# A graph attention stage beside a small mixture of experts: the order of TensorE, DVE and ACT written out tile by tile

## The chip, the cores and the metric

The kernel runs on one core of one Trainium2 chip. It is one launch that computes four graph layers with a feed-forward layer after each. The metric is the time of one execution on the device in microseconds (us). The time before the change is the median of three runs. Besides these there is one execution taken by the hardware profiler, from which all views come; its own time is given in the table below.

A core has five engines that work beside each other: TensorE (PE, matrix products, with the loading of weights shown apart as PEld), VectorE (DVE), ScalarE (ACT), GpSimd (POOL) and SyncE (SP, which here only issues transfers). TensorE writes to PSUM, from which DVE and ACT read. Engines wait for each other by semaphores.

## The reference

There are N = 3125 nodes with 256 features and E = 53125 edges, sorted by the node `dst` at which they end. The change touches the first graph layer and the feed-forward layer after it; six more layers follow, and each reads the whole result of the one before.

```python
def _L0_gnn_ref(nfeat, attn_bias, Wq, Wk, Wv, Wo, src, dst):
    ...
    q = (nfeat @ Wq.T).reshape(n, HEADS, HEAD_DIM) / SCALING
    k = (nfeat @ Wk.T).reshape(n, HEADS, HEAD_DIM)
    v = (nfeat @ Wv.T).reshape(n, HEADS, HEAD_DIM)
    attn = jnp.einsum('ehd,ehd->eh', k[src], q[dst])
    attn = attn + attn_bias
    m = jax.ops.segment_max(attn, dst, num_segments=n)
    a = jnp.exp(attn - m[dst])
    s = jax.ops.segment_sum(a, dst, num_segments=n)
    a = a / s[dst]
    out = jax.ops.segment_sum(v[src] * a[:, :, None], dst, num_segments=n)
    return out.reshape(n, FEAT) @ Wo.T
...
x = x + _L0_gnn_ref(_layernorm(x, axis=-1), edge_attr_8, L0_gnn_Wq, L0_gnn_Wk, L0_gnn_Wv, L0_gnn_Wo, src, dst)
x = x + _L0_ffn_ref(_layernorm(x, axis=-1)[None], L0_ffn_sW1, ..., L0_ffn_gb)[0]
```

So each edge takes the key and the value of its source node and the query of its target node, in 8 heads of 32; a softmax runs over the edges of a target, and the weighted values are summed by target. The feed-forward layer normalizes a row and adds a shared network of three layers (256, 256, 128, 256) and a mixture of four small experts (256, 128, 64, 256), of which each row keeps the two with the highest gates; their weights are a softmax of these two gates.

## The kernel before

**Tiles.** The 3125 nodes are 25 tiles (`T`) of 125 (`P`). The edges that end in one tile are a window of at most 18 chunks (`WC`) of 128 edges. A window is handled in three pieces of six chunks (`PC`), and a piece is one buffer `kv` of 128 edges by 6 chunks, which holds the weights of the heads, a column of ones, the keys (columns `KO` to `VO`) and the values (from `VO`). Before the loop, keys and values of all nodes are written to memory (`kv_d`).

**What is done for a tile**, with the lines of the kernel before:
- `gathered` (L1660): six indirect transfers by POOL's queue bring the rows of a piece; five may be under way, and each has to follow the fifth before it. There are seven buffers `kv`. DVE then sets the column of ones (L1666).
- `one_hot` (one operation of DVE, L282) marks for each edge its target; SP loads the tile's normalized rows `lt_t` and the edges' biases `eb_t`. `one_hot_turned` turns the marks on TensorE (18 transposes, L1826) and ACT copies them out in three parts (L1827, `oht`).
- `queries` (L1815 to L1819): a product on TensorE, scaled by ACT, and split into three bf16 parts so that their sum is exact: a cast on DVE, a difference on DVE, a cast on ACT, a difference on DVE.
- `logits(p)` for each piece: nine blocks `qx` for a tile, of two chunks each, are products of `oht` and the three query parts (six matmuls, L1840). DVE multiplies the keys by each block (L1843), and per piece sums over each head (L1844). Two PSUM buffers `qx` take turns.
- `sums_of`: DVE adds the bias (L1850), ACT takes a first exponential at an eighth of the size (L1853, `el`), TensorE sums it by target (18 matmuls, L1856), DVE copies (L1858).
- `weights_of`: DVE makes from these sums a level for each target (L1864), TensorE hands it to the edges (18 matmuls, L1868), DVE subtracts and clips (L1869, L1871), ACT takes the exponentials into `kv` (L1873, three).
- `weighted`: for each piece DVE multiplies values by weights (L1878), ACT casts the marks to float (L1883, `oh_f`), TensorE sums six chunks into `acc` (L1885), which has one buffer. The column of ones makes the number of edges `deg` of each target beside it.
- `normed`, `normed_turned`, `projected`: DVE copies `deg` (L1890), takes inverses (L1892, L1893) and scales (`ao`, L1895); TensorE turns it (L1902), ACT copies (L1904), TensorE multiplies by `Wo`, DVE adds to `x` (L1909).

**The loop.** It runs 26 times, t = 0 to 25, and each time works on three tiles: `now` (logits), `before` (the tile ahead of it: weights, values, projection) and `after` (the one behind it: marks and queries). After the loop the counts `deg` are used for the next stages.

**The experts beside it.** A tile whose attention is done is ready for the experts. `Experts0` takes the tiles in pairs, as a generator `group`; each call of `more.step` runs it to its next `yield`, with one buffer for each name and one PSUM buffer `tr`. A pair has 14 steps: normalize (DVE statistics and a square root by ACT, L230 to L242), turn (L250), gates (from L719), turned gates, two halves of `s1`, then `s2`, the experts two by two with `e1`, `pair` and `pick` (L885 is the product with the gates), and the output product and addition to `x` (L893) for each tile. The loop calls `beside()` eight times per iteration. `evacuate` (copies out of PSUM, L224 and L226) and `relu_into` (L779 and L781) go to DVE and ACT in turn. There are 11 pairs inside the loop. `group`'s weights are loaded at its start, and DVE adds two of their biases (L834) before the first pair.

**Windows.** From t = 5 on the loop also calls `windows.next()` once an iteration: steps that prepare indices for later graph stages, among them two indirect transfers on POOL's queue that wait for SP's load of pointers.

**What sets the order.** The program text gives an order, and the tile scheduler of the language decides from it, with estimates of its own, in which order the instructions of each engine are put. So matmuls of the experts, logits and `acc` come out mixed. What is queued on one engine then runs in that fixed order.

Of the kernel before, what the change touches and what calls it, by code (L numbers as in the profile page):

```python
# [10 lines left out]
F32 = mybir.dt.float32  # L11
# [24 lines left out]
H, HD = 8, 32  # L36
# [34 lines left out]
def gnn_ffn_kernel(ctx: ExitStack, tc: tile.TileContext, a, out: bass.AP):  # L71
# [156 lines left out]
    def normalize(pool, dst, src, n, tag, scale=None):  # L228
# [8 lines left out]
        nc.scalar.activation(rs[:, :n], rs[:, :n], AF.Sqrt)  # L237
        nc.vector.reciprocal(rs[:, :n], rs[:, :n])
# [6 lines left out]
    def transposed(psum, dst, src, n, relu=False):  # L245

        for k in range(2):
# [5 lines left out]
            if not relu:  # L253
                evacuate(dst[:, k, :n, :], of)
            elif k:
                nc.scalar.activation(dst[:, k, :n, :], of, AF.Relu)
            else:
                nc.vector.tensor_scalar(dst[:, k, :n, :], of, 0.0, None, ALU.max)

# [458 lines left out]
    def gates(pool, psum, lt, n, wg, bias, ne, top, ahead=None):  # L718


# [20 lines left out]

        nc.vector.tensor_tensor(g, ps[:, :n * ne].rearrange("p (i e) -> p i e", e=ne),
                                bias.unsqueeze(1).to_broadcast([P, n, ne]), ALU.add)
        exp_from_max()
        normed(g)
# [5 lines left out]
        ranks(pool, first, g, n, ne, ahead)  # L751
        nc.vector.tensor_scalar(first, first, 2.5, None, ALU.is_lt)
        if top == "softmax":
            exp_from_max()
        nc.vector.tensor_mul(g, g, first)
# [3 lines left out]
    class TurnedGates:  # L759
# [7 lines left out]
        def __call__(self, psum, g, n, ne):  # L767
# [5 lines left out]
            evacuate(wt[:ne, :n, :].rearrange("e i p -> e (i p)"), ps[:ne, :n * P])  # L773
            return wt

    def relu_into(dst, ps, bias):
        turn[0] ^= 1
        if turn[0]:
            nc.vector.tensor_scalar(dst, ps, bias, 0.0, ALU.add, ALU.max)  # L779
        else:  # L780
            nc.scalar.activation(dst, ps, AF.Relu, bias=bias)  # L781
# [11 lines left out]
    class Experts0:  # L793


        def __init__(self, pools):
# [4 lines left out]
            with weights_of_pool(wpool, (SLOT0, D)):  # L801
                self.group = experts0_by(pool, psum, 2)
# [11 lines left out]
    def experts0_by(pool, psum, most):  # L814
# [30 lines left out]

        def group(t0, n):
            ln = pool.tile([P, most, D], F32, name="ln")
            normalize(pool, ln, x[:, t0:t0 + n, :], n, "a")
            yield
            lt = pool.tile([128, 2, most, P], F32, name="lt")  # L850
            transposed(psum, lt, ln, n)
            yield
            g = gates(pool, psum, lt, n, gw, gb, 4, "softmax", ahead)
            yield
            gt = turned_gates(psum, g, n, 4)
            c = n * P

            def hidden(name, m, terms, bias):
                ps = tr()
                product(ps[:m, :c], terms)  # L860
                relu_into(name, ps[:m, :c], bias)
# [11 lines left out]
            for p in range(2):  # L873
# [8 lines left out]
                relu_into(e2[:, p, :c], ps2[:, :c], cols2[:, p:p + 1])  # L882
                ps = tr()
                product(ps[:, :c], [(pick[:, p, :], fan(gt[:, :n, :]))])
                nc.vector.tensor_mul(e2[:, p, :c], e2[:, p, :c], ps[:, :c])  # L885
                yield
            for i in range(n):
# [4 lines left out]
                        + [(e2[:, p, at], ew3[:, p, :]) for p in range(2)])  # L892
                nc.vector.tensor_add(xt, xt, po)  # L893
                yield
# [732 lines left out]
    def attention(windows, experts):  # L1627
# [10 lines left out]
        with ExitStack() as es:  # L1638
# [16 lines left out]
            def gathered(at):  # L1655
# [10 lines left out]
                nc.vector.memset(kv[:, :, KO - 1:KO], 1.0)  # L1666
# [130 lines left out]
            def one_hot(t):  # L1797
                s = Tile()
                s.t, s.kv = t, begun if t == 0 else []
                oh = pool.tile([128, WC, HC], BF16, name="oh")  # L1800
                one_hots(oh, row_h[:, t * WC:(t + 1) * WC, :], iota_h)
                s.oh = oh[:, :, :P]
# [6 lines left out]
            def queries(s):  # L1809

                ps = psum.tile([P, D], F32, name="sm")
                product(ps, [(s.lt[:, k, :], wq[:, k, :]) for k in range(2)])
                s.q = pool.tile([P, 3, D], BF16, name="q_t")
                q = pool.tile([P, D], F32, name="q")
                nc.scalar.activation(q, ps, AF.Copy, scale=float(HD) ** 0.5)  # L1815
                nc.vector.tensor_copy(s.q[:, 0, :], q)
                nc.vector.tensor_sub(q, q, s.q[:, 0, :])
                nc.scalar.copy(s.q[:, 1, :], q)
                nc.vector.tensor_sub(s.q[:, 2, :], q, s.q[:, 1, :])  # L1819

            def one_hot_turned(s):
                s.oht = pool.tile([P, WC, 128], BF16, name="oht")
                for c0 in range(0, WC, PC):
                    ps = psum.tile([128, 1024], BF16, name="sm")
                    for c in range(PC):
                        nc.tensor.transpose(ps[:P, c * 128:(c + 1) * 128], s.oh[:, c0 + c, :], ident_h)  # L1826
                    nc.scalar.copy(s.oht[:, c0:c0 + PC, :].rearrange("d c e -> d (c e)"),  # L1827
                                   ps[:P, :PC * 128])
                s.l = pool.tile([128, WC, H], F32, name="l")

            def logits(s, p):

                if p == len(s.kv):
                    s.kv.append(gathered(s.t * WC + p * PC))
                kv = s.kv[p]
                for c0 in range(0, PC, 2):
                    ps = psum.tile([128, 2, D], F32, name="qx", bufs=2)
                    for c in range(2):
                        for k in range(3):
                            nc.tensor.matmul(ps[:, c, :], s.oht[:, p * PC + c0 + c, :], s.q[:, k, :],  # L1840
                                             start=(k == 0), stop=(k == 2))
                    k_ = kv[:, c0:c0 + 2, KO:VO]
                    nc.vector.tensor_mul(k_, k_, ps)  # L1843
                nc.vector.tensor_reduce(  # L1844
                    s.l[:, p * PC:(p + 1) * PC, :],
                    kv[:, :, KO:VO].rearrange("p c (h d) -> p c h d", h=H), AX.X, ALU.add)

            def sums_of(s):
# [3 lines left out]
                el = pool.tile([128, WC, H], BF16, name="el")  # L1852
# [666 lines left out]
```

## Time and profile before

| what | us |
|---|---|
| median of three runs | 3411.0 |
| lowest and highest of them | 3409.88, 3411.66 |
| the profiled execution, its time | 3415.6 |
| the profiled execution, its span | 3413.8 |
| from the span's start to the first matmul of the attention (L1840) | 119.5 |
| from there to the last matmul of `acc` (L1885) | 797.3 |
| from there to the span's end | 2497.0 |

The profiler's own time is 0.13% above the median. The span is what the trace covers, from its first to its last instruction.

The next answer gives the busy time of each engine in these three stretches; the number in brackets counts instructions. It is followed by PE's granted clock as a share of full speed, the busy share of the transfer engines and what they moved.

```profile
0.00:119.50 119.50, 71.80 (x241) 37.55 (x242) 62.20 (x231) 23.98 (x60) 31.94 (x40) 0.87 0.65 189
119.50:916.80 797.30, 708.14 (x4621) 550.44 (x4620) 610.90 (x1319) 222.20 (x445) 451.50 (x442) 0.92 0.53 153
916.80:3413.80 2497.00, 2352.99 (x11729) 1858.21 (x11727) 1069.06 (x3358) 787.83 (x1492) 196.53 (x157) 0.96 0.36 98
```

The columns after the stretch and its length are PE, PEld, DVE, ACT and POOL. In the attention stage PE is busy in 708 of 797 us, DVE in 611, POOL in 452, most of it with the gathers, ACT in 222. [...]

The largest groups of that stage, by line, are these; after the bar stand the busy time and the mean of one instruction in ns, then how long the engine was idle just before them and what released it.

```profile
L1885 PE MATMUL acc<-kv,oh_f 128*125 128x265 f32 x900 | 224.9, 412 | 14.6 <-DVE kv L1878 14.6
L1840 PE MATMUL qx<-q_t,oht 125*128 125x256 bf16 x1350 | 216.2, 296 | 53.9 <-DVE kv L1843 41.2 <-DVE q_t L1819 5.7 <-ACT q_t L1818 5.5
...
L1843 DVE TENSOR_TENSOR kv<-kv,qx 128x512 f32<-128x512 f32 x225 | 150.7, 679 | 26.2 <-PE qx L1840 24.7 <-DMA kv<-kv_d,src_w 0.7
...
L1844 DVE TENSOR_REDUCE l<-kv 128x48 f32<-128x1536 f32 x75 | 130.9, 1745 | 0.2
L1878 DVE TENSOR_TENSOR kv<-kv 128x1536 f32<-128x1536 f32 x75 | 128.4, 1750 | 0.6 <-ACT kv L1873 0.6
```

PE stands idle for 53.9 us ahead of logit matmuls, mostly until DVE has freed a block `qx`, and for 14.6 us ahead of `acc`.

### The profile page before, as it was taken

How to read it: one execution, taken by the hardware profiler on the slowest of the kernel's cores; microseconds unless marked ns; L12 is line 12 of the kernel's file. 1: busy time of each engine (PE TensorE's matmuls, PEld its weight loads, DVE VectorE, ACT ScalarE, POOL GpSimd, SP SyncE). 2: the span in 40 equal slices, each digit the busy share in tenths (PEclk: the TensorE clock that was granted, in tenths of full speed). 3: DMA queues.
4: the chain of work that ended last, by engine and by line, in shares of the span. 5: the costliest groups of instructions: out<-in, count | busy, mean ns of one | idle time of the engine just before them, and what ended most of it. 6: DMA issues, size and time to landing. Idle time of an engine off the chain costs nothing. (4 is left out here: it accounts for less than half of the span.)

```text
span 3413.8 us, 45380 instructions
## 1 busy us (share of the span) xinstructions
PE 3132.9 (92%) x16587; PEld 2446.2 (72%) x16587; DVE 1742.2 (51%) x4905; ACT 1034.0 (30%) x1996; POOL 680.0 (20%) x639
## 2 busy tenths in 40 slices
PE   6688998998888899999996999979999999999898
PEld 2466776777677789898885888868755555579666
DVE  6577778777697534344674122155521111355662
ACT  1222332332255423232331222234423232332120
POOL 1665564655100000000134333200000000000000
PEclk9789998999889999999997999989999999999997
DMA  5755554555256734444344666553200000043001
GB/s 165 235 172 150 160 163 143 160 165 144 61 165 215 192 99 119 102 108 110 91 123 133 185 178 180 167 137 103 69 19 10 10 19 10 7 122 100 21 1 39
DMA packets 253208, 388.23 MB, mean 114 GB/s; under 512 B 41454, under 2 KB 201069, under 8 KB 252973
## 3 DMA queue, kind: packets, MB, share of 16 engines
q1 hardware_dynamic: 184090, 226.68, 23.3%
q0 software_dynamic: 54064, 141.25, 15.3%
q10 hardware_dynamic: 14819, 17.27, 1.9%
q8 instruction: 134, 2.20, 0.3%
q14 instruction: 101, 0.83, 0.1%
HBM read 314.47 MB, written 70.58 MB: 113 GB/s over the span
## 5 line engine op out<-in xcount | busy, mean ns | idle before, releaser
L2222 PE MATMUL agg<-cnt_f,hp 125*128 125x500 f32 (+1 forms) x3500 | 733.1, 369 | 22.2 <-ACT hp L2163 22.0
L2222 PEld LDWEIGHTS agg<-cnt_f,hp 125*128 125x128 f32 x3500 | 635.5, 189 | 103.2 <-ACT hp L2163 23.1
L1660 POOL DMA_INDIRECT kv<-kv_d,src_w x450 | 450.9, 1002 | 281.5 <-PE acc L1885 140.5
L2200 ACT CAST cnt_f<-blk 125x500 fp32r<-125x500 bf16 (+1 forms) x435 | 245.5, 565 | 518.4 <-PE agg L2222 496.7
L2200 DVE CAST cnt_f<-blk 125x500 fp32r<-125x500 bf16 (+1 forms) x440 | 185.5, 423 | 265.5 <-PE agg L2222 221.6
L1382 DVE SCALAR_TENSOR_TENSOR x<-po,gall,x 125x256 f32<-125x256 f32 x200 | 93.8, 484 | 417.5 <-PE po L266 416.9
L1376 ACT ACTIVATE h<-hid_ps,shift,scale 128x500 f32<-128x500 f32 (+1 forms) x224 | 161.9, 723 | 376.0 <-PE hid_ps L266 375.5
L1840 PE MATMUL qx<-q_t,oht 125*128 125x256 bf16 x1350 | 216.2, 296 | 53.9 <-DVE kv L1843 41.2
L1885 PE MATMUL acc<-kv,oh_f 128*125 128x265 f32 x900 | 224.9, 412 | 14.6 <-DVE kv L1878 14.6
L1885 PEld LDWEIGHTS acc<-kv,oh_f 128*125 128x125 f32 x900 | 178.5, 201 | 54.2 <-DVE kv L1878 18.5
L1840 PEld LDWEIGHTS <-oht 125*128 125x128 bf16 x1350 | 138.2, 105 | 100.4 <-issue 50.6
L266 PE MATMUL po<-wslot,h 128*125 128x256 f32 x800 | 203.0, 386 | 0.1
L266 PEld LDWEIGHTS po<-wslot,h 128*125 128x125 f32 x800 | 145.0, 187 | 75.2 <-ACT h L1376 27.0
L266 PE MATMUL hid_ps<-h,wslot 128*128 128x500 f32 (+1 forms) x448 | 193.8, 556 | 4.1 <-ACT h L1376 0.6
L266 PE MATMUL hid_ps<-xe,wslot 128*128 128x256 f32 x832 | 187.3, 383 | 1.8 <-DVE xe L1214 1.8
L1072 POOL DMA_INDIRECT xs_d<-r_l,pos x50 | 60.2, 1204 | 645.3 <-DVE r_l L1068 567.1
L266 PE MATMUL hid_ps<-v_rows,wslot 128*128 128x500 f32 (+1 forms) x448 | 186.8, 537 | 0.0
L1225 ACT ACTIVATE hid<-hid_ps,wslot 128x256 f32<-128x256 f32 x208 | 98.5, 475 | 286.8 <-PE hid_ps L266 286.8
L266 PE MATMUL po<-wslot,hid 128*128 128x256 f32 x832 | 184.5, 378 | 0.0
L266 PEld LDWEIGHTS hid_ps<-xe,wslot 128*128 128x128 f32 x832 | 150.7, 191 | 33.4 <-ACT hid L1225 4.1
L266 PEld LDWEIGHTS po<-wslot,hid 128*128 128x128 f32 x832 | 155.7, 189 | 21.8
L1843 DVE TENSOR_TENSOR kv<-kv,qx 128x512 f32<-128x512 f32 x225 | 150.7, 679 | 26.2 <-PE qx L1840 24.7
(512 smaller groups left out, 4625.8 us busy)
## 6 DMA issues: line engine op xcount, KB each, us to landing
wslot<-in_ex_W SPq DMA_DIRECT2D x52, 1024.0 KB
blk<-an_d SPq DMA_DIRECT2D x60, 546.9 KB
blk<-at_d SPq DMA_DIRECT2D x40, 546.9 KB
blk<-an_d SPq DMA_DIRECT2D x45, 410.2 KB
at_d<-ab SPq DMA_DIRECT2D x25, 683.6 KB
an_d<-an SPq DMA_DIRECT2D x25, 683.6 KB
blk<-at_d SPq DMA_DIRECT2D x30, 410.2 KB
kv<-kv_d,src_w POOLq DMA_INDIRECT x450, 3.7
```

The source lines that it names most:

```text
L266: nc.tensor.matmul(ps, l, r, start=(bias is None and i == 0), stop=(i == last))
L1072: st = nc.gpsimd.indirect_dma_start(out=xs_d, in_=l2[:, i, :].bitcast(I32), in_offset=None, out_offset=bass.IndirectOffsetOnAxis(ap=self.p ...
L1225: nc.scalar.activation(hid[:, m, :], ps[:, :BLK], AF.Gelu, bias=c[:, 4 + m:5 + m])
L1376: nc.scalar.activation(dst[:, m, :c], ps[:, :c], AF.Relu, bias=shift[:, l, col:col + 1], scale=scale[:, l, col:col + 1])
L1382: nc.vector.scalar_tensor_tensor(x[:, t0 + i, :], po, gating.all[:, t0 + i, e:e + 1], x[:, t0 + i, :], ALU.mult, ALU.add)
L1660: got = nc.gpsimd.indirect_dma_start(out=kv[:, c, KO:], out_offset=None, in_=kv_d, in_offset=bass.IndirectOffsetOnAxis(ap=src_i[:, at + c: ...
L1840: nc.tensor.matmul(ps[:, c, :], s.oht[:, p * PC + c0 + c, :], s.q[:, k, :], start=(k == 0), stop=(k == 2))
L1843: nc.vector.tensor_mul(k_, k_, ps)
L1885: nc.tensor.matmul(s.acc[:, :D + H + 1], of[:, c, :], kv[:, c, AO:VO], start=(p == 0 and c == 0), stop=(p == 2 and c == PC - 1))
L2200: to(f[:, :n, :], part[0][:, :n, m % MB, :])
L2222: nc.tensor.matmul(ps[f][:, :c], hp[:, m, k, f * 128:(f + 1) * 128], got[:, :c], start=(m == 0 and k == 0), stop=(m == T - 1 and k == 1))
```

## The change

The attention loop is put inside `tc.manual_schedule` for PE, DVE and ACT: on these three engines the order of the program text is the order in which instructions are queued. POOL's and SP's queues are not named in it. The text of an iteration is new, as the function `iteration(t, b, n, a)`, where `b`, `n` and `a` are the former `before`, `now` and `after`:

- `logits` is cut into `asked` (one block of six matmuls), `multiplied` (one product on DVE) and `summed` (one sum per piece). `weighted` and `collected` are the values of one piece and its third of `acc`; between the thirds stand products and blocks of the next tile's logits. The first two blocks of tile `a` are asked at the end of the iteration before.
- `casts` makes the three `oh_f` of tile `b` at the head of the iteration, in three buffers.
- `sums_of` and `weights_of` are cut too; the first exponential of a tile is at the head of the next iteration.
- A piece is gathered (`more_rows`) after each `collected`; seven are begun ahead of the loop. The column of ones is set in `weighted`, no longer at the gather.
- In `queries` ACT reads the product twice and writes the first part and the float copy; the first cast on DVE is gone. The differences follow later, in `second_part` and `third_part`.
- The copy of `deg` goes from DVE to ACT.
- `brought` issues SP's two loads of tile `a` at the head of the iteration, ahead of `one_hot`, which was with them before.
- `q`, `ao` and `at` have one buffer instead of two.
- `Experts0` asks for `on_act`: the copies of `lt` and of the turned gates and all its relus are by ACT. `normalize`, `transposed` and `gates` become generators, so that a pair has 22 steps; `beside()` is called 11 times per iteration. After the square root of `normalize`, ACT takes one exponential of a single number (`warm`).
- `Windows` has one more `yield`, before its copies out of PSUM.

```diff
@@ normalize_by, transposed_by, gates_by
         nc.scalar.activation(rs[:, :n], rs[:, :n], AF.Sqrt)
+        yield
         nc.vector.reciprocal(rs[:, :n], rs[:, :n])
...
             if not relu:
-                evacuate(dst[:, k, :n, :], of)
+                (to or evacuate)(dst[:, k, :n, :], of)
...
+            yield
...
+        yield
         nc.vector.tensor_tensor(g, ps[:, :n * ne].rearrange("p (i e) -> p i e", e=ne),
                                 bias.unsqueeze(1).to_broadcast([P, n, ne]), ALU.add)
         exp_from_max()
+        yield
         normed(g)
...
         ranks(pool, first, g, n, ne, ahead)
+        yield
         nc.vector.tensor_scalar(first, first, 2.5, None, ALU.is_lt)
         if top == "softmax":
             exp_from_max()
+        yield
         nc.vector.tensor_mul(g, g, first)
         normed(g)
@@ relu_into, experts0_by
-        if turn[0]:
+        if turn[0] and not on_act:
             nc.vector.tensor_scalar(dst, ps, bias, 0.0, ALU.add, ALU.max)
...
+        by_act = nc.scalar.copy if on_act else None
+        warm = pool.tile([1, 1], F32, name="warm", bufs=1)
+
         def group(t0, n):
             ln = pool.tile([P, most, D], F32, name="ln")
-            normalize(pool, ln, x[:, t0:t0 + n, :], n, "a")
+            for _ in normalize_by(pool, ln, x[:, t0:t0 + n, :], n, "a"):
+                nc.scalar.activation(warm, ones[:1, :1], AF.Exp)
+                yield
+            lt = pool.tile([128, 2, most, P], F32, name="lt")
+            yield from transposed_by(psum, lt, ln, n, to=by_act)
+            g = yield from gates_by(pool, psum, lt, n, gw, gb, 4, "softmax", ahead)
+            gt = turned_gates(psum, g, n, 4, by_act)
             yield
...
                 product(ps[:, :c], [(pick[:, p, :], fan(gt[:, :n, :]))])
+                yield
                 nc.vector.tensor_mul(e2[:, p, :c], e2[:, p, :c], ps[:, :c])
                 yield
...
-                nc.vector.tensor_add(xt, xt, po)
                 yield
+                nc.vector.tensor_add(xt, xt, po)
@@ the attention's functions
+            def more_rows():
+                if len(pieces) < T * (WC // PC):
+                    pieces.append(gathered(len(pieces) * PC))
...
+                nc.scalar.activation(s.q[:, 0, :], ps, AF.Copy, scale=float(HD) ** 0.5)
+                nc.scalar.activation(s.rest, ps, AF.Copy, scale=float(HD) ** 0.5)
+
+            def second_part(s):
+                nc.vector.tensor_sub(s.rest, s.rest, s.q[:, 0, :])
+                nc.scalar.copy(s.q[:, 1, :], s.rest)
+
+            def third_part(s):
+                nc.vector.tensor_sub(s.q[:, 2, :], s.rest, s.q[:, 1, :])
...
+            def casts(s):
+                s.of = []
+                for p in range(WC // PC):
+                    of = pool.tile([128, PC, P], F32, name="oh_f", bufs=3)
+                    nc.scalar.copy(of, s.oh[:, p * PC:(p + 1) * PC, :])
+                    s.of.append(of)
...
+            def weighted(s, p):
+                kv = piece(s, p)
+                nc.vector.memset(kv[:, :, KO - 1:KO], 1.0)
+                nc.vector.tensor_mul(
...
+            def collected(s, p):
+                if p == 0:
+                    s.acc = psum.tile([P, 512], F32, name="acc", bufs=1)
+                for c in range(PC):
+                    nc.tensor.matmul(s.acc[:, :D + H + 1], s.of[p][:, c, :], piece(s, p)[:, c, AO:VO],
+                                     start=(p == 0 and c == 0), stop=(p == 2 and c == PC - 1))
+                more_rows()
 
             def normed(s):
-                nc.vector.tensor_copy(deg[:, s.t:s.t + 1], s.acc[:, H:H + 1])
+                nc.scalar.copy(deg[:, s.t:s.t + 1], s.acc[:, H:H + 1])
```

The new iteration, without the conditions that leave out a missing tile (each call stands under `if b`, `if n` or `if a` by its argument):

```python
            def iteration(t, b, n, a):
                first_powers(b); beside()
                casts(b); multiplied(n, 0); powers_summed(b)
                multiplied(n, 1); asked(n, 2); beside()
                levels(b); levels_spread(b)
                multiplied(n, 2); asked(n, 3); weights_of(b); asked(n, 4); beside()
                summed(n, 0); beside(); beside()
                for p in range(3):
                    weighted(b, p); collected(b, p)
                    multiplied(n, 3 + p); asked(n, 5 + p)
                summed(n, 1); one_hot(a)
                multiplied(n, 6); asked(n, 8)
                one_hot_turned(a); queries(a)
                normed(b); multiplied(n, 7); normed_turned(b); beside()
                multiplied(n, 8); second_part(a); beside()
                summed(n, 2); projected(b); beside()
                third_part(a); added(b); beside()
                asked(a, 0); asked(a, 1); beside()
                if t >= Windows.TB: windows.next()
                beside()
```

Within a pair's iterations, the eleven steps of the first (odd t) are the normalization to its root, the two turned halves with the rest of the normalization, the gates' product, the first exponential, its sum with the ranks, the second exponential, the turned gates, the two halves of `s1` and `s2`; those of the second begin with the first `e1`.

## The prediction

> **What bounds the kernel now.** I read the page first: TensorE (PE) works in 92% of the span, so stages add up, and a stage ends when its PE work and PE waits end.
>
> ```profile
> span 3413.8 us, 45380 instructions
> ...
> PE 3132.9 (92%) x16587; PEld 2446.2 (72%) x16587; DVE 1742.2 (51%) x4905; ACT 1034.0 (30%) x1996; POOL 680.0 (20%) x639
> ...
> PE   6688998998888899999996999979999999999898
> ...
> DVE  6577778777697534344674122155521111355662
> ...
> PEclk9789998999889999999997999989999999999997
> ```
>
> The change touches one stage. The attention's matmuls (lines L1840, L1885) run from 119.5 to 916.8 us, slices 2 to 11. There PE has 8 or 9 tenths, DVE 7, and the clock is not always full. Next, stretches of about one tile:
>
> ```profile
> core 0: us, PE busy (x) PEld busy (x) DVE busy (x) ACT busy (x) POOL busy (x), PEclk, DMA share, GB/s
> 380.00:412.00 32.00, 27.32 (x174) 21.59 (x173) 24.93 (x54) 7.19 (x15) 14.56 (x15) 0.89 0.42 125
> 412.00:444.00 32.00, 30.60 (x208) 23.29 (x207) 23.54 (x47) 11.33 (x22) 21.38 (x23) 1.00 0.63 185
> 444.00:476.00 32.00, 26.30 (x198) 21.04 (x196) 25.32 (x58) 7.98 (x17) 19.56 (x16) 1.00 0.44 123
> ```
>
> Two kinds alternate, since a pair of tiles shares one group of expert work. I call B the one at 412 (experts' hidden layers, PE full), A the other (normalization, gates, first layer; PE waits). Marking tiles by the activation `el` (L1853): it starts at 390.45, 419.93 and 454.32, so A takes 29.5 and B 34.4 by that mark; over the 22 tiles from 197.56 to 896.37 a pair takes 698.8/11 = 63.5 us. Third, PE and ACT in order of time:
>
> ```profile
> 399.71 0.43 PE L250 MATMUL tr<-ident,ln 125*128 125x125 f32 x2 [0.25 <-ACT lt L226]
> 400.66 1.03 PE L266 MATMUL tr<-wslot,lt 128*125 128x4 f32 x8 [0.51 <-DVE lt L224]
> 402.32 9.99 PE L1885 MATMUL acc<-kv,oh_f 128*125 128x265 f32 x36 [0.63 <-DVE kv L1878]
> ...
> 431.21 8.30 PE L1885 MATMUL acc<-kv,oh_f 128*125 128x265 f32 x36 [0.33 <-DVE kv L1878]
> ```
>
> ```profile
> 390.45 0.32 ACT L1853 ACTIVATE el<-l 128x144 bf16<-128x144 f32 x1 [7.76 <-DVE l L1850]
> 390.79 1.28 ACT L237 ACT_TABLE_LOAD   x1
> 394.77 0.20 ACT L237 ACTIVATE rsa<-rsa 125x2 f32<-125x2 f32 x1 [2.69 <-DVE rsa L236]
> 395.00 1.28 ACT L1873 ACT_TABLE_LOAD   x1
> 396.29 0.52 ACT L1873 ACTIVATE kv<-l 128x48 f32<-128x48 f32 x3
> ...
> 407.05 0.82 ACT L1883 CAST oh_f<-oh 128x750 f32<-128x750 bf16 x1 [7.39 <-PE acc L1885]
> ...
> 413.13 2.20 ACT L1827 COPY oht<-sm 125x768 bf16<-125x768 bf16 x3
> ```
>
> Short gaps of 0.2 to 0.6 us stand before each link of the gates' chain, and the same 36 matmuls take 8.30 us in B and 9.99 after such gaps. The scheduler has put other PE work into most gaps.
>
> [...]
>
> **PE's own work, part by part.** It is the same in both kernels. Intervals from start to start at clock 1.00 (412 to 452 us): 6 `qx` matmuls 0.65, a third of `acc` 2.72, 18 transposes 1.05, queries 0.87, sums 1.0, levels 0.45, a hidden layer 0.95, `pair` 0.57, `pick` 0.52, projection 0.87, one output product 1.73. Summed over the written order, an iteration has 9 x 0.65 + 3 x 2.72 + 4.5 for the rest of the attention = 18.5; the experts add 4.4 in A (22.9) and 10.6 in B (29.1). So 52.0 a pair; now 63.5, hence 11.5 of idle and half clock to win, at most 11 x 11.5 = 126 us.
>
> Saved on DVE: the copies and relus of L224 and L779 that go to ACT (0.41 to 0.47 each, about 6 a pair), the first cast of the queries (0.30) and the copy of deg (0.16): some 3.5 us a pair. DVE then has about 25.6 in A, 22 in B, under PE's pair sum. That buys nothing by itself: what counts is who waits in the fixed order. What is moved on the queues I cost at nothing. The memsets are 0.06 each. The gathers of a piece (6 of 1.0 us on POOL) are issued when a third of `acc` frees it and land a tile ahead, covered by seven buffers, over 30 us; without that cover a late piece would cost 6. The windows' index gathers now stand behind 108 gathers in POOL's queue instead of 90, each after SP's pointer load of the iteration before. SP's two loads a tile go to the head of the iteration; the tile is used one iteration later.
>
> **Iteration A, by hand** (0 = last output product of B done; DVE operations start 0.08 before the former ends; hand-overs 0.05 to 0.1):
> - DVE adds to x (0.41), then `l` (0.39), ACT `el` (0.32), only then the sums on PE, and nothing stands between on PE: idle 1.4.
> - DVE's statistics (0.4 + 0.2, twice) stand before the first product, which frees the third `qx`: 0.5. The square root waits for its table (1.28) and `ln` for it: first transposition at 4.2, idle 0.8.
> - ACT then loads the exp table (1.28, the new `warm`) and makes three casts (2.3) before it may copy `lt`: done at 6.8; second half after three exps, 7.75. PE waits 0.6 and 0.7. In before, casts ran late, beside `acc`.
> - Gates end at 8.8. DVE, idle since 7.4, makes three small steps and one product of the values (1.75) before the first third of `acc`: 11.2. PE idle 2.5.
> - Thirds and logits run without gaps to 22.0, the transposes to 23.05. ACT copies them (2.3), makes both query activations (0.8), and only then the copy of deg; DVE's `inv` waits for that copy[...]. `acc` is done at 20.9, `inv` starts at 25.5: DVE is idle 5.6 us with two logit products behind it. PE: 0.4 for a buffer, 2.1 for `ao`, 0.7 for its copy.
> - DVE goes on in series: 0.8 normalization, two products 1.2, ranks 1.45, second part 0.34, 0.4, a sum 1.66, gates' end 0.8: 32.2. PE waits there for the gates from 28.2: 4.1, then 0.6 for their copy (one buffer `tr`).
> - s1, s2 and B's first layer follow each other through that buffer: twice 0.8 for relu (0.47) and hand-overs.
> Idle: 1.4+0.5+0.8+0.6+0.7+2.5+0.4+2.1+0.7+4.1+0.6+1.6 = 16.0. A = 38.9.
>
> **Iteration B.** The same deg chain: PE 0.4 and 2.4; 0.75 for the buffer behind `pick`, 0.75 for the first product of the values, 0.8 for one relu: 5.1. B = 34.2. A pair 73.1, against 63.5.
>
> **Clock.** Not in this sum. In A PE is idle for most of 6 to 11 and 24 to 33 us[...]. At 120 to 156 us of before PE is 62% busy and the clock 0.81. At 0.80 in A, 16 of 41 us run at half and lose 16 x 0.6 / 2 = 4.8; B at 0.92 loses 2.4. About two thirds lie on the path: 5 (2 to 9). A pair then takes 78.1, +14.6; 11 pairs +161.
>
> **Both ends.** Tile 0 still waits until 133 us for the experts' weights (DVE, DMA `in_eb`); the two tiles without experts take about 26 us each by the same chain; my sum reaches the third mark 3 us late. The last iteration has no logits, so the deg copy waits for nothing; the next stage's work still fills it: 0. More steps of the windows fall into the next stage: -3 to +8, taken as 0. Total +164 on the profiled execution's 3415.6 (its span 3413.8 and 1.8 around it), 3580; that execution lies 0.13% over the median of 3411.0, so on the median I forecast 3575.
>
> **Rivals.**
> 1. The gaps are shorter than laid out (loads pulled ahead, clock kept full): pair 66 to 74; at 70 it is 6.5 x 11 + 3 = +75, 3486. For it: gaps of 1.6 us at 452 did not bring the clock down. Against: the waits are in the built order.
> 2. The clock falls further, pair over 83; at 84, 20.5 x 11 + 3 = +229, 3640. For it: 40% idle in A.
> 3. Faster. One mechanism: DVE's relief lets the thirds and logits keep PE full, A and B near their PE sums; at 58 a pair it saves 5.5 x 11 = 61: 3350. It decides once idle and half clock fall under 11.5 a pair. For it: `acc`, the costliest group, now has logits between its thirds. Against: these gaps were only 0.3 to 0.6 us before, and it must lose half of the 21 laid out (16.0 and 5.1). A layout by hand adds up many small hand-overs, and if each is too long the sum is too, so this keeps some weight.
> 4. No change: pair 63 to 64, 3411. A coincidence.
> That the order is not what it says can be left out: the built order on the three engines follows the text.
>
> **Numbers.** Forecast (pair 74 to 83) 0.54, rival 1 0.22, rival 2 0.07, rival 3 0.15, rival 4 0.02. Slower 0.83, same 0.02, faster 0.15; 0.2% (7 us) is about what can be told from no change. Range 3440 to 3640 (pairs of about 66 to 84): it leaves out rivals 3 and 4 and half of rival 2, 0.20 in all.
>
> **What would show it.** Right: `el` at alternating distances of about 42 and 36 us; DVE idle about 5 us before `inv`, released by ACT's deg copy; PE waiting 4 us for the gates' transposes in A; PEclk near 0.8 there; attention ending near 1080 us; later stages unchanged. Wrong: `inv` released by `acc` itself, or PEclk 1.00 and pairs under 63.

## The result, and the profile after

The changed kernel takes 3584.5 us (median of four runs, 3580.1 to 3586.6) against 3410.6 for the kernel before: a ratio of 1.0508, with a 95% interval of 1.049 to 1.0526. It is slower, by 174 us on the medians; the two profiled executions are 3580.1 and 3415.6 us, 164.5 apart.

The page of the changed kernel, in the lines that were shown of the kernel before:

```profile
span 3577.8 us, 45312 instructions
...
PE 3182.3 (89%) x16587; PEld 2463.2 (69%) x16587; DVE 1719.9 (48%) x4778; ACT 1076.1 (30%) x2138; POOL 681.2 (19%) x639
...
PE   6588787888778889999999699979999999999898
...
DVE  6565665565667863434467412116631111254662
...
PEclk9788888888888999999999799999999999999998
```

PE does as many instructions as before, in 49 us more of busy time, and works in 89% of the span instead of 92%. From the second slice to the thirteenth PE has mostly 7 or 8 where it had 8 or 9, the granted clock 8 where 9 was frequent, and DVE 5 or 6 where it had 7. What follows has much the same digits, moved to the right by about one slice.

The same three stretches as in the table before (PE, PEld, DVE, ACT and POOL busy, clock, share of the transfer engines, GB/s):

```profile
0.00:113.60 113.60, 68.02 (x224) 34.87 (x225) 60.91 (x224) 21.23 (x55) 29.42 (x38) 0.88 0.66 191
113.60:1079.00 965.40, 765.94 (x4636) 573.58 (x4634) 587.48 (x1170) 260.21 (x578) 455.26 (x445) 0.86 0.45 127
1079.00:3577.80 2498.80, 2348.35 (x11730) 1854.79 (x11729) 1071.53 (x3384) 794.61 (x1506) 196.51 (x157) 0.97 0.36 98
```

The attention begins 5.9 us earlier, lasts 168.1 us longer, and what follows takes 1.8 us more: the whole difference of the spans, 164.0, lies in the stage that was rewritten. There PE is busy 57.8 us longer for the same matmuls, at a granted clock of 0.86 instead of 0.92 (one matmul of `acc` takes 432 ns on average instead of 412), and is idle 199 us instead of 89.

One iteration of each kind, from one start of the activation `el` to the next (the first is A, with the experts' normalization and gates, the second B, with their hidden layers):

```profile
435.16:477.85 42.69, 32.13 (x180) 23.43 (x179) 28.19 (x67) 12.09 (x28) 18.54 (x20) 0.76 0.47 135
477.85:513.12 35.27, 30.43 (x198) 23.15 (x199) 22.76 (x42) 9.46 (x23) 16.92 (x16) 1.00 0.39 112
```

All pairs are alike: A lasts 42.6 to 43.8 us, B 35.3 to 36.0. Over 22 tiles, from 199.13 to 1058.06 us, a pair takes 78.1 us; it was 63.5. In B PE is busy for 30.4 of 35.3 us at full clock. A has fewer matmuls and takes longer, with a clock of 0.76; PE is idle for 10.6 us of it (42.69 - 32.13).

PE in order of time in that iteration A; the bracket gives the idle time before a line and who ended it:

```profile
445.57 5.66 PE L1942 MATMUL acc<-kv,oh_f 128*125 128x265 f32 x12 [2.33 <-DVE kv L1933]
...
451.74 2.85 PE L1942 MATMUL acc<-kv,oh_f 128*125 128x265 f32 x12
...
455.08 2.85 PE L1942 MATMUL acc<-kv,oh_f 128*125 128x265 f32 x12
...
460.48 1.13 PE L276 MATMUL sm<-wq,lt_t 128*125 128x256 f32 x4 [0.19 <-ACT oht L1853]
463.48 0.40 PE L1959 MATMUL sm<-ident,ao 125*128 125x125 f32 x2 [1.88 <-DVE ao L1952]
464.35 1.67 PE L276 MATMUL sm<-wo,at 128*125 128x256 f32 x4 [0.46 <-ACT at L1961]
469.08 0.58 PE L791 MATMUL tr<-ident,g 125*4 125x125 f32 x2 [3.06 <-DVE g L752]
470.10 2.03 PE L276 MATMUL tr<-lt,wslot 128*128 128x250 f32 x4 [0.45 <-ACT g_turned L794]
```

The first third of `acc` takes 5.66 us after a gap of 2.33, at a granted clock of 0.51 (445.5 to 451.3 us); the second takes 2.85 for the same twelve matmuls, at 0.99 (451.3 to 465.0 us). So behind this gap stands a second loss, of 2.8 us, at half clock. In this iteration the granted clock is 0.50 to 0.55 in three stretches: 437.3 to 441.1, 445.5 to 451.3 and 465.0 to 474.8 us. Each begins behind gaps that stand close together (1.18 and 0.38 us, 0.46 and 2.33, 1.88 and 0.46), and the third stretch also holds the gap of 3.06. Not every gap has such a loss behind it: in the iteration B that follows PE waits as long for `ao`, with little other idle time around, and the clock is 1.00 throughout.

```profile
502.80 0.40 PE L1959 MATMUL sm<-ident,ao 125*128 125x125 f32 x2 [1.88 <-DVE ao L1952]
```

After the thirds PE waits for `ao`, and then for the gates. Both come from DVE, and DVE in turn waits, as its line in this iteration and the answer about the line of `inv` say (in the answer: us in total, times):

```profile
462.48 0.17 DVE L1949 TENSOR_SCALAR inv<-acc 125x8 f32<-125x8 f32 x1 [6.21 <-ACT deg L1947]
```

```profile
  ACT deg L1947: 146.3, 25
```

So before each of the 25 tiles' `inv` DVE stands still, for 5.9 us on average, until ACT has copied `deg`. `inv` reads eight other columns of `acc`; why it has to wait for that copy the trace does not show. ACT's order shows why the copy is late (the copy of the marks, the two query activations, and only then `deg`):

```profile
459.62 2.20 ACT L1853 COPY oht<-sm 125x768 bf16<-125x768 bf16 x3 [15.54 <-PE sm L1852]
461.70 0.42 ACT L1862 ACTIVATE q_t<-sm 125x256 bf16<-125x256 f32 x1
461.97 0.42 ACT L1863 ACTIVATE q<-sm 125x256 f32<-125x256 f32 x1
462.24 0.21 ACT L1947 COPY deg<-acc 125x1 f32<-125x1 f32 x1
```

`acc` was complete near 458 us, where its last twelve matmuls end (they begin at 455.08 and take 2.85 us), and the copy of `deg` begins 4.3 us later.

### The profile page after: what moved, and what is told of

The parts are those of the page before. It is cut to its first block, busy times and chain, and to the rows that moved or that the text cites. A ratio compares the mean times of both kernels' runs of the same rounds, so it can differ in the third digit from the quotient of the medians.

```text
span 3577.8 us, 45312 instructions
## 1 busy us (share of the span) xinstructions
PE 3182.3 (89%) x16587; PEld 2463.2 (69%) x16587; DVE 1719.9 (48%) x4778; ACT 1076.1 (30%) x2138; POOL 681.2 (19%) x639
## 3 DMA queue, kind: packets, MB, share of 16 engines
q0 software_dynamic: 54064, 141.25, 14.6%
## 4 chain that ended last, share of the span: by engine, by line
PE 80%; DVE 8%; DMA 4%; ACT 3%; issue 3%; POOL 1%; SPq 0%; ACTq 0%; DVEq 0%; POOLq 0%
PE agg L2338 20%; PE po L276 18%; PE hid_ps L276 14%; PE acc L1942 7%; PE tr L276 6%; PE qx L1878 5%; DMA kv<-kv_d,src_w 2%; PE row L276 1%; PE tok L1561 1%; POOL kv L1685 1%; PE tr L259 1%; PE tr L2426 1%; PE pair L276 1%; ACT oht L1853 1%; DVE kv L1933 1%
## 5 line engine op out<-in xcount | busy, mean ns | idle before, releaser
L1942 PE MATMUL acc<-kv,oh_f 128*125 128x265 f32 x900 | 248.3, 432 | 39.6 <-DVE kv L1933 30.5
L1878 PE MATMUL qx<-q_t,oht 125*128 125x256 bf16 x1350 | 205.7, 306 | 19.5 <-DVE kv L1884 14.8
```

What stands on the lines that cost most here:

```text
L1878: nc.tensor.matmul(ps[:, c, :], s.oht[:, 2 * i + c, :], s.q[:, k, :], start=(k == 0), stop=(k == 2))
L1942: nc.tensor.matmul(s.acc[:, :D + H + 1], s.of[p][:, c, :], piece(s, p)[:, c, AO:VO], start=(p == 0 and c == 0), stop=(p == 2 and c == PC - 1))
```

## The experiments

The first theory: the loss is the written order, by its waits, and the largest of them is DVE's behind ACT's copy of `deg`. The first rival: the other edits cost, whoever orders them. The second rival: DVE's idle time is cover, and taking the `deg` wait away brings nothing.

The first nine runs stood on chips on which the kernel before takes 3773 to 3808 us instead of 3411; each is given as a ratio to the kernel before on its own chip, with its 95% interval.

**deg by DVE.** One line goes back to what it was:

```diff
-                nc.scalar.copy(deg[:, s.t:s.t + 1], s.acc[:, H:H + 1])
+                nc.vector.tensor_copy(deg[:, s.t:s.t + 1], s.acc[:, H:H + 1])
```

> One edit to the changed kernel: the copy of deg is by DVE again, ahead of inv on the same engine. Theory (the waits of the fixed order make the loss, and the wait of DVE behind ACT's deg copy is the largest of them): inv starts about 4.5 us earlier in both kinds of iteration, PE's wait of 1.9 us for ao goes in both, and in the first kind most of the 3.1 us wait for the gates' transposes; with the clock about 8 us a pair, so about 90 us in all: 3465 to 3515. Rival (DVE's idle time is cover, and what ends an iteration is the chain of the experts through one buffer, or the low clock that follows other gaps): within 25 us of 3584.

3862.0 us, 1.016 (1.0117 to 1.0202) of the kernel before, which took 3808.4 there. The times that were expected belong to a chip like that of the first result; the changed kernel was not timed on this one, so this run and the next three are read against the table further down.

**The order left to the scheduler**, all other edits kept:

```diff
-            with tc.manual_schedule(engines={mybir.EngineType.PE, mybir.EngineType.DVE, mybir.EngineType.Activation}):
+            with ExitStack():
```

> One edit to the changed kernel: the fixed order is taken away, so the scheduler orders PE, DVE and ACT from the same new text, with all other edits left in (ACT's copies and relus, 22 steps, casts at the head, early gathers, one buffer for q, ao and at, deg copied by ACT). Theory (the loss is the order): a pair comes back to 60 to 66 us, 3375 to 3445. Rival (the other edits cost, whoever orders them: ACT has more to do in front of what PE waits for, and single buffers bind): over 3500.

3767.9 us, 0.9902 (0.9866 to 0.9938).

**A step of the experts earlier**, alone and together with `deg` by DVE:

```diff
+                beside()
                 if b:
                     normed(b)
...
                     normed_turned(b)
-                beside()
```

> One edit to the changed kernel: the sixth step of the experts in an iteration (gates' sum and ranks in the first kind, a hidden layer in the second) stands before normed instead of after normed_turned. Theory: in the first kind DVE does some 2 us of it in its idle time before inv, so the gates' transposes come 2 us earlier; in the second kind PE gets a hidden layer to do while it waits 1.9 us for ao. About 4 us a pair with the clock: 3520 to 3560. Rival (the chain through the buffer of the experts' PSUM decides, which only moves): within 15 us of 3584.

> Both edits of the two runs before: deg copied by DVE, and the sixth step before normed. Theory: the gains overlap in the gates' wait (only 3.1 us of it is there to go), so less than their sum: 3440 to 3500. If the waits were independent, the sum of both gains; if the deg wait is not the cause, no better than the step alone.

3884.9 us, 1.0196 (1.0153 to 1.0239), and with both edits 3857.5 us, 1.0134 (1.0094 to 1.0173). The interval of the earlier step overlaps that of the changed kernel in the table below, so no gain of it is shown. With both edits the time can't be told from that of `deg` by DVE alone, and it is 27 us below the step alone. The next four runs have the changed kernel beside them:

> The changed kernel unaltered, as the mark for the runs beside it: the runs of the first four stood on a chip where the kernel before took 3808 us, and the changed one had no time there. If this chip is like that of the first result, 3570 to 3595 beside 3411; if like the other, what the change costs there decides how the ratios of the first four are read: theory (the order's waits cost about 160 us on any chip) gives a ratio of 1.03 to 1.05.

> deg copied by DVE again, alone, beside the changed kernel on the same chip. Theory: 70 to 110 us below the changed kernel, by an inv that starts about 4.5 us earlier. Rival (DVE's idle time is cover): within 25 us of it.

> The fixed order taken away, all else of the change left in. Theory (the loss is the order): 0.985 to 1.005 of the kernel before. Rival (the other edits cost): over 1.02 of it.

**A rewritten order.** `r4_order` has `deg` by DVE and this iteration (conditions left out as before; `cast` is one of the three casts):

```python
multiplied(n, 0); beside(); powers_summed(b)
multiplied(n, 1); asked(n, 2); levels(b); levels_spread(b); beside()
multiplied(n, 2); asked(n, 3); weights_of(b); cast(b, 0); beside()
asked(n, 4); cast(b, 1)
weighted(b, 0); collected(b, 0); multiplied(n, 3); asked(n, 5); beside()
weighted(b, 1); cast(b, 2); collected(b, 1)
summed(n, 0); multiplied(n, 4); asked(n, 6)
weighted(b, 2); collected(b, 2); multiplied(n, 5); asked(n, 7); beside()
one_hot(a); multiplied(n, 6); asked(n, 8); normed(b); beside()
normed_turned(b); one_hot_turned(a); projected(b)
multiplied(n, 7); multiplied(n, 8); beside()
queries(a); beside(); second_part(a); summed(n, 1); beside()
third_part(a); added(b); asked(a, 0)
summed(n, 2); first_powers(n); beside()
asked(a, 1); windows.next(); beside()
```

> A fixed order again, but rewritten after the waits that the changed kernel's trace shows: deg by DVE; the first exponential at the end of the iteration before; the gates' steps between the thirds of acc, not ahead of them and not behind the deg chain; casts one by one; ao turned ahead of the marks. By hand: first kind 27 to 30 us, second kind 30 to 32, so a pair of 57 to 62 with the clock, against 63.5 in the kernel before and 78 in the changed one: 0.98 to 1.00 of the kernel before. Rival (a fixed order can't keep PE fed, since hand-overs of small steps add up wherever they stand): a pair over 68, more than 1.015 of the kernel before.

| on a chip where the kernel before takes 3773.4 us | us | ratio | 95% |
|---|---|---|---|
| changed kernel | 3860.0 | 1.0236 | 1.0206 to 1.0265 |
| deg by DVE | 3857.6 | 1.0225 | 1.0191 to 1.0258 |
| order left to the scheduler | 3746.6 | 0.9927 | 0.9904 to 0.995 |
| rewritten order | 3727.7 | 0.9899 | 0.9863 to 0.9936 |

Two things follow for these chips. The other edits cost nothing there: with the order left to the scheduler they are 0.7% below the kernel before, so the first rival falls, and the written order makes the changed kernel 3.1% slower than the same text in the scheduler's order (1.0236 / 0.9927 = 1.031, from 1.026 to 1.036 by the ends of the two intervals). And a written order need not lose: the second one, which has `deg` by DVE too, can't be told from the scheduler's order by the intervals. On a chip like that of the first result the order left to the scheduler was not run, so that the 174 us there come from the order alone is not shown directly.

Two expectations failed. The changed kernel loses 87 us here, not the 160 that were to hold on any chip. And `deg` by DVE brings 2.4 us, less than the spread of either kernel's runs, as its rival said. The same kernel once more,

> deg copied by DVE again, once more, for a chip on which the kernel before takes about 3411 us as in the first result (the two before took 3808 and 3773, with waits of ACT and DVE that the trace can't place). Theory: there inv starts about 4.5 us earlier, PE's waits for ao (1.9 us, both kinds) go and most of the 3.1 us for the gates' transposes: 70 to 110 us below the changed kernel, ratio to the kernel before 1.018 to 1.03. Rival (DVE's idle time is cover, or the low clock eats the gain): ratio 1.043 or more.

fell on such a chip again: 3866.9 us, 1.0172 (1.0152 to 1.0191). The traces show what took the place of the wait. ACT in an iteration A of the first run with `deg` by DVE:

```profile
786.36 0.80 ACT L1853 COPY oht<-sm 125x768 bf16<-125x768 bf16 x1 [19.68 <-remote]
792.80 0.80 ACT L1853 COPY oht<-sm 125x768 bf16<-125x768 bf16 x1 [5.64 <-remote]
799.86 0.80 ACT L1853 COPY oht<-sm 125x768 bf16<-125x768 bf16 x1 [6.26 <-remote]
```

The 18 transposes that these copies read had ended by 783.1 us, and yet the copies stand 6 to 7 us apart; the releaser is called remote, which means that the trace names no engine of this core. `deg` and `inv` were done near 781 us, and DVE went on, only to stand 16.9 us before the difference that makes the second query part, whose input ACT was to deliver (in the whole run DVE waits in this way 20 times, 249.4 us in total). So there the 6 us are saved by DVE and lost by ACT. Most of this waiting falls into the time in which POOL issues gathers (774 to 797 us). To have the chain without gathers, the last three runs leave them out.

**Without gathers.** In the changed kernel, with `deg` by DVE, and with the rewritten order:

```diff
-                for c in range(PC):
-                    got = nc.gpsimd.indirect_dma_start(
...
+                r0 = at * 128 % 2048
+                nc.sync.dma_start(kv[:, :, KO:], kv_d[r0:r0 + 128 * PC].rearrange("(p c) d -> p c d", c=PC))
```

> The changed kernel with the gathers of POOL taken out: each piece is filled by one plain transfer of 768 neighbouring rows from SP's queue, so that keys and values are those of other nodes than the edges' sources. The same bytes are moved and all else stays. Theory (on the chips of the later runs, where ACT and DVE show waits of several us that the trace marks as remote, these come with the bursts of 18 gathers): the waits go, and the marks of el stand 42 to 44 and 35 to 36 us apart as in the first result, a pair near 78. Rival (the waits belong to the chip, not to the gathers): distances of 50 and 45 stay.

> The same without gathers, and deg copied by DVE. Theory of the deg chain: DVE's wait before inv falls from 6 to under 2 us, PE's waits for ao and for the gates' transposes go in large part, and a pair is 6 to 9 us shorter than in the run without gathers beside it. Rival (DVE's idle time is cover): less than 2 us shorter.

> The same without gathers, with the rewritten order. By hand 57 to 62 us a pair, against 63.5 in the kernel before in its first profile. Rival (small hand-overs add up in any fixed order): over 66.

This time the kernel before took 3407.4 us, as in the first result. So whether gathers cause the remote waits was not tried after all; but the three give the chain on a chip like the first.

| without gathers | us | ratio, 95% | a pair, from 22 tiles |
|---|---|---|---|
| changed kernel | 3634.9 | 1.0663, 1.0632 to 1.0694 | 78.1 |
| deg by DVE | 3549.5 | 1.0412, 1.0382 to 1.0442 | 71.1 |
| rewritten order | 3490.9 | 1.024, 1.0199 to 1.0282 | 65.5 |

The pair of the first is the 78.1 us of the changed kernel with its gathers, so gathers are hidden in it. The 50 us above 3584.5 are elsewhere: from the last matmul of `acc` to the end its profile has 48 us more than the changed kernel's, and the other two of this group 46 and 42. These runs compute other values, and a later stage sends rows to experts by value: it does more work here, 896 matmuls of each of its two products instead of 832 (below, the first of them in the changed kernel and in the first run without gathers), and PE has 16723 matmuls in all instead of 16587. The ratios in the table contain this. So the three are compared with each other by their times, and with the two kernels by their pairs only.

```profile
L276 PE MATMUL hid_ps<-xe,wslot 128*128 128x256 f32 x832 | 186.6, 382 | 1.8 <-DVE xe L1239 1.8
L276 PE MATMUL hid_ps<-xe,wslot 128*128 128x256 f32 x896 | 203.1, 385 | 1.8 <-DVE xe L1239 1.8
```

`deg` by DVE takes 7.0 us from a pair and 85.4 us from the time: the theory said 6 to 9 us, the rival less than 2. DVE's wait there is down to 1.6 us a tile, now for `acc` itself. The iterations A and B of the three, in the columns used above:

```profile
408.33:444.21 35.88, 30.60 (x198) 23.26 (x199) 20.81 (x35) 9.35 (x22) 0.00 (x0) 1.00 0.38 136
444.21:486.57 42.36, 31.94 (x180) 23.47 (x179) 27.93 (x67) 12.09 (x27) 0.00 (x0) 0.76 0.34 118
```

```profile
411.17:448.88 37.71, 29.66 (x180) 22.27 (x179) 28.08 (x68) 11.93 (x26) 0.00 (x0) 0.86 0.37 133
448.88:482.08 33.20, 30.25 (x198) 23.25 (x199) 22.86 (x43) 9.11 (x21) 0.00 (x0) 1.00 0.40 147
```

```profile
462.12:494.19 32.07, 27.78 (x196) 22.35 (x196) 27.41 (x68) 11.27 (x24) 0.00 (x0) 0.95 0.44 154
494.19:527.78 33.59, 29.09 (x190) 21.98 (x190) 21.04 (x36) 9.82 (x23) 2.74 (x2) 0.99 0.44 151
```

The first fence, of the changed kernel, shows B and then A; the other two show A and then B. With `deg` by DVE, A loses 4.6 us, B 2.7; in A PE's idle time falls from 10.4 to 8.1 us, and the clock rises from 0.76 to 0.86. What PE still waits for in A, with `deg` by DVE:

```profile
438.16 1.13 PE L276 MATMUL sm<-wo,at 128*125 128x256 f32 x4 [0.89 <-ACT at L1956]
441.04 0.38 PE L791 MATMUL tr<-ident,g 125*4 125x125 f32 x2 [1.75 <-DVE g L752]
```

The wait of 1.9 for `ao` is gone, that for the gates has fallen from 3.1 to 1.75. The rewritten order then wins another 5.6 us a pair, at clocks of 0.95 and 0.99; which of its moves brings how much was not tried. (Its `el` stands at another place of the iteration, so its A and B are not the same stretches of work as theirs.) A pair of 65.5 us lies above the 57 to 62 that were worked out for it, just below the 66 of its rival, and 2.0 above the 63.5 of the kernel before. The order keeps all other edits but the copy of `deg`, so on such a chip, and without gathers, most of the 14.6 us a pair go with the order and that copy, not with them. But it is not shown to beat the kernel before there: with its real gathers it was not run on such a chip, and 144 us below the changed kernel's 3584.5 (3634.9 - 3490.9) would be about 3440, an estimate. On the chip with 3773.4 us, on which it ran, its time is 1.0% below that of the kernel before and 3.4% below that of the changed one.

## Why the prediction was right

The forecast was 3575 us from +164 on the profiled execution; measured are 3584.5 and +164.5. The place, the main wait and the sum were right; the split of the loss between idle time and clock was not, and there luck helped. By its steps:

- **Where.** Only the attention stage was to change, and later stages not. It changed by +168.1 (and -5.9 at its start), the rest by 1.8.
- **A pair.** 78.1 was forecast and 78.1 measured; A about 42 (42.6 to 43.8), B about 36 (35.3 to 36.0). The marks alternate as foretold. The eleven pairs bring +160.1 us where +161 was forecast.
- **Both ends.** The third mark was to come 3 us late and comes 1.6 late; the stages behind the attention were to change by nothing and take 1.8 us more.
- **The deg chain.** DVE was to be idle 5.6 us before `inv`, released by ACT: 5.9. PE was to wait 2.1 for `ao` and 0.7 for its copy: 1.88 and 0.46. That this wait reaches PE, and is not cover, is shown by the two runs without gathers, one with it and one without: 7.0 us of a pair, about half of the 14.6 that the change costs (78.1 - 63.5). On the chips where the kernel before takes about 3800 us the same edit shows no such gain.
- **The gates.** 4.1 us before their transposes and 2.5 before the first third of `acc` were forecast; 3.06 and 2.33 came.
- **The casts.** Two waits of 0.6 and 0.7 were laid out where ACT makes its casts ahead of the copies of `lt`. In the iteration shown only one of 0.46 us is there. This term was too large.
- **The split between idle and clock.** The idle gaps of A were laid out as 16.0, and in the iteration shown PE is idle for 10.6. The clock was taken as 0.80 in A and 0.92 in B; it was 0.76 and 1.00. PE is busy 32.1 us in A for the 22.9 us of work at full clock, so the work takes 9.2 us longer than that, where 4.8 were laid out for half clock and two thirds of them put on the path. So idle was taken too large by 5.4 us and the clock too small by about 6: 19.8 us are lost in A (42.7 - 22.9), against about 19 in the forecast (16.0 and 3.2). It may be that a PE at half clock spends in work a part of the time that it would have waited; no run separates the two. That the sum fitted so well is in part luck: these two errors offset each other.
- **When the clock falls.** The prediction laid the half clock where PE is idle for most of a stretch, at 6 to 11 and 24 to 33 us of A. In the traces no single long gap stands ahead of it. In the kernel before, no gap from 380 us to the slow `acc` at 402 is over 1.62 us, yet the clock is 0.51 from 397.0 to 399.7 us and 0.64 to 0.75 from 402.3 to 408.0. In this A no gap is over 3.06, and the clock is 0.50 to 0.55 in the three stretches named above, each behind several shorter gaps. What rule the clock follows these traces do not show.
- **Work on the queues at nothing.** The early gathers, SP's loads and the memsets were put at zero. The run without gathers has the same pair, which agrees for the gathers on a chip like the first. On the other chips a pair of the changed kernel takes 95.6 us instead of 78.1, most of the waits that the trace can't place fall where gathers are issued (174 of 214 us, last section), and nothing there tests this term.
- **Rival 3**, that DVE's relief would let PE run full at 58 us a pair, asked for half of the laid out 21 us of idle to vanish. In the iterations shown 15.4 us are there (10.6 and 4.8), and the clock in A is lower than laid out.

What the prediction did not weigh is the new text without its fixed order: left to the scheduler, it was 0.7 and 1.0% faster than the kernel before on the two chips where it ran.

## What to carry to other kernels

When an order is written out by hand, follow each value from the engine that makes it to the engine that needs it, through the queue of every engine between: a copy of 0.2 us put behind 3 us of other work on ACT held DVE for 6 us in each tile and, on a chip like that of the first result, made about half of the loss. Move only what shortens such a chain: here DVE was busy for 23 us less in the stage (587.5 instead of 610.9), and the stage took 168 us longer. And where gaps in front of TensorE stand close together, count them as longer than they are: in the iteration A shown, the clock behind them was 0.50 to 0.55 for 3.8 to 9.8 us (5.66 us for what takes 2.85), while in B it stayed at 1.00 around a gap of 1.88 us within busy work.

## What the runs showed of the hardware

For the first nine runs the kernel before took 3773 to 3808 us on the chips they stood on, for the first result and the last three runs 3407 to 3411. On the former chips a pair takes 95.6 us with the changed kernel (78.1 with the first result) and 86.8 with the rewritten order (65.5 without gathers), and ACT and DVE show waits of up to 27 us whose releaser the trace calls remote; the trace of the changed kernel with the first result, and those of the last three runs, have none. Two of the largest in the changed kernel on such a chip (us, times, longest):

```profile
DVE inv L1949 <- remote: 48.6, 4, 13.6
ACT oht L1853 <- remote: 47.4, 18, 11.1
```

The two traces of the changed kernel are of the same program, and their spans differ by 244 us (3821.8 - 3577.8). Of these, 40 lie ahead of the first logit matmul, while the first seven pieces are gathered, 199 between it and the last matmuls of `acc`, and 5 in all that follows. In the changed kernel's trace on the chip with 3773.4 us, 174 of the 214 us of remote waits of ACT and DVE up to the end of the attention fall into the bursts in which POOL issues gathers. These bursts fill somewhat less than half of the stage: by an estimate about 550 of 1164 us, from the 24.2 us that the 18 gathers from 799.85 us on take, the 408 gathers that follow the first seven pieces, and the stage's length (965.4 + 199). For POOL's indirect transfers the page gives a time from issue to landing with the first result (3.7 us for a gather), but none in any of the first nine runs, so a releaser may also be missing from the record.

Whether the gathers make these waits stays open: most of the waits fall where gathers are issued, but the runs that left the gathers out fell on a chip without such waits. What can be said is that an order's worth differs between the two kinds of chip: the rewritten order gains 132 us over the changed kernel on the one (3860.0 - 3727.7) and, without gathers, 144 on the other, but `deg` by DVE alone gains 2 on the one and 85 on the other.
